# Two blocks moved into the paired stage, an early load, and two norms by halves in a two-layer sparse graph kernel

## The chip, the core and the metric

The kernel runs on one core of one Trainium2 chip. The metric is device time in microseconds for one execution. Five engines work side by side, each through its own queue in order: TensorE (PE in the profile), VectorE (DVE), ScalarE (ACT), GpSimd (POOL) and SyncE (SP). In this kernel SP issues the plain transfers, and POOL issues the indirect ones (gathers and scatters by row number). [...]

## What is computed

Two layers over 2708 nodes with 1024 features. Layer 0 is attention over each node's neighbours with a residual and a layer norm, layer 1 is a sum over neighbours, a projection, a residual and a layer norm.

```python
q = x @ W_q.T + b_q;  k = x @ W_k.T + b_k;  v = x @ W_v.T + b_v
z = (q @ k.T / sqrt(1024)) * adj
z = where(z == 0.0, -10000.0, z)
x = layernorm(x + relu(softmax(z) @ v))      # layer 0
x = layernorm(x + adj @ (x @ weight) + bias) # layer 1
```

The adjacency matrix is sparse and holds zeros and ones. A node without neighbours has the same value in every place of its row of z, so its attention is the plain mean over all nodes.

## The kernel before, in words

Everything is float32. The first stage lists each row's neighbours, sorts the rows by their number of neighbours, and folds the two weights of the scores into one matrix m, so that a score is the product of a row y = x m + constant with a row of x. Sorting makes 22 blocks of at most 128 rows, in two families (blocks 0 to 7 and 8 to 21). `SLOTS` (L32) gives for each sorted block how many neighbours its rows have at most: 15 in block 0, 11 in block 1, down to 0 in block 21, which is the list `last` (L98). Very connected rows are split into shares (the "hub").

**The y stage** (`y_block`, L288) goes over the rows in their natural order: 16 matmuls of 512 columns for a block of 128 rows, two additions on VectorE, a store to DRAM. Each block's part of xT comes by `load_x` (L272) into one of three buffers. Block 21 has only 20 rows. Its tile is cleared by GpSimd, then loaded (L278 to L280), and its products are laid out in four column groups (L305). ACT sums each block's columns (`column_sums`, L330) and from these sums comes the mean of x (L294).

**Attention jobs** (`attend`, `attend_one`, `attend_shares`) belong to sorted blocks. A job gathers the block's y rows (L343) and, slot by slot, neighbour rows of x (L349) into nine rotating tiles g, computes scores on VectorE (L792), a softmax, and the weighted sum of the same x rows in a tile r (L847, L849). A block that takes y rows from the second family needs the whole y stage to be over. The list `late_jobs` holds these.

**The projection of layer 0** turns r through PE (`flip`, L709, or `flip_shares`, L720, for block 0) and multiplies it with the 1024x1024 weight W_v. There are three ways. A single block ("v" step, `project`, L734) takes 16 matmuls of 512 columns. The mean (`project_mean`, L745) is one row for all rows of block 21. A pair of blocks ("p" step, `pair_products`, L990) takes seven products of half by half instead of eight, 28 matmuls in place of 32. For that it needs four combinations of the turned halves (`turn_pair`, L954, tile `s_all`) and the weight differences `wv_t`, four operations on VectorE (L1107 to L1110), the first of which changes a quarter of the weights in place. They lie in the buffers of m, so the y stage and the single projections of the original weights must come before them.

After the products, `finish0` (L879, single) or `finish_pair` (L1040) applies ReLU, adds the x row, and calls `norm` (L767): a mean from the accumulated sums, squares on ACT over the whole row (L775), Ln and Exp on ACT with four small VectorE operations for the inverse root, and the scaling of the row on ACT (L788). The row is scattered to the DRAM tensor x1 (L703). The tile t of a single block comes from the pool `wp` with two buffers; in a pair the first block's t comes from `wp`, the second's from a pool that opens when the y stage ends (`xb_pools[0]`), with two buffers too.

**The order** is written out by hand. `steps` (L1060) lists y blocks, single projections and pairs; the loop at L1090 walks through it, and a credit of estimated microseconds decides how many attention jobs are emitted before each step. A turn is emitted up to one step ahead of its projection (L1120). A scheduler then places instructions in the engines' queues by this order as their priority. `high_priority(URGENT)` marks the additions that free a PSUM bank. `follow` puts one instruction behind another, with a semaphore or, with `same=True`, only in the order of one engine's queue.

**Layer 1** starts when every row of x1 is scattered. `units` (L1192) lists one single block and ten pairs. `sum_rows` (L1197) gathers x1 rows (L349) and adds them up on VectorE (L1209, L1211), `turn1` turns them, `gather_x1` (L1214) fetches the residual row onto the bias, `work1` (L1235) multiplies and `finish1` (L1221) norms and scatters to the output. Before the loop, the sums of units 0, 1 and 2 are emitted, and in the loop those of unit i + 3.

```python
steps += [("v", b) for b in [1, 0] + last] + [("p", pair) for pair in pairs]
```

Of the kernel before, what the change touches and what calls it, by code (L numbers as in the profile page):

```python
# [20 lines left out]
P = 128  # L21
# [59 lines left out]
def sparse_part(ctx, tc, x, xT, adj, wqT, wkT, wvT, bq, bk, bv, w1, b1, out):  # L81
# [29 lines left out]
    with es:  # L111
# [158 lines left out]
        xts = []  # L270

        def load_x():  # L272
            b = len(xts)
            if b == NB:
                return
            r0, n = b * P, rows[b]
            xt = xa.tile([P, DC, P], F32, name="xt", bufs=3)
            if n < P:  # L278
                nc.gpsimd.memset(xt, 0.0)
            nc.sync.dma_start(out=xt[:, :, :n], in_=xT[:, r0:r0 + n].rearrange("(c p) n -> p c n", p=P))  # L280
            xts.append(xt)
# [48 lines left out]
        def column_sums(b, behind=None):  # L330
            for c in range(DC):
                put = nc.scalar.activation(junka, xts[b][:, c, :], AF.Copy, accum_out=xs[:, c, b:b + 1])  # L332
                if behind is not None and c % 2 == 0:
                    follow(put, behind[c // 2])
# [432 lines left out]
        def norm(t, sm, n, sm2=None):  # L767
# [21 lines left out]
            return end  # L789

        def score(yg, xg, s, n):
            nc.vector.scalar_tensor_tensor(junkv[:n], yg[:n, :D], scale, xg[:n], op0=ALU.mult, op1=ALU.mult,  # L792
                                           accum_out=s)
# [85 lines left out]
        def finish0(b, po, xr):  # L879
            n = rows[b]  # L880
            t = wp.tile([P, D], F32, name="t")
            for h in range(NH):
                hs = slice(h * HALF, (h + 1) * HALF)
                with tc.high_priority(URGENT):
                    nc.vector.tensor_add(t[:n, hs], po[h][:n], bias_bc[:n, hs])
            sm = stat.tile([P, 1], F32, name="sm")
            nc.vector.scalar_tensor_tensor(t[:n], t[:n], 0.0, xr[:n], op0=ALU.max, op1=ALU.add, accum_out=sm[:n])
            end = norm(t, sm, n)
            scatter(x1_d[:, :], b, n, t, "x1")
            return end  # L890
# [61 lines left out]


        def turn_pair(flips, pool):  # L954
# [12 lines left out]
            nc.vector.tensor_sub(S[2], a11, a21)  # L967
            nc.vector.tensor_sub(S[3], a12, S[1])
            return A, S
# [60 lines left out]
        def project_pair(pair, A, S):  # L1030
            ts = [(xb_pools[0] if k else wp).tile([P, D], F32, name="t", bufs=2) for k in range(2)]
            bias = halves_of(bias_bc)

            def whole(k, h, acc, what):
                add(halves_of(ts[k])[h], acc, what)

            pair_products(A, S, wv_q, wv_t, [bias, bias], [halves_of(t) for t in ts], whole, pair == pairs[-1])
            return ts

        def finish_pair(pair, ts):  # L1040
            for k, (b, t) in enumerate(zip(pair, ts)):
                xr, sums = pair_x[b], [stat.tile([P, 1], F32, name=f"sm{h}", bufs=6) for h in range(NH)]
                for h in (0, 1) if k == 0 else (1, 0):
                    th = halves_of(t)[h]
                    nc.vector.scalar_tensor_tensor(th, th, 0.0, halves_of(xr)[h], op0=ALU.max, op1=ALU.add, accum_out=sums[h])
                norm(t, sums[0], P, sums[1])
                scatter(x1_d[:, :], b, P, t, "x1")
# [7 lines left out]
        jobs = [6, 5, 4, 3, 2, 2, 1, 1, "hub", "hub", 0, 0, 0]  # L1055
        pairs = [(7, 20), (19, 18), (17, 8), (16, 11), (15, 10), (9, 14), (13, 12)]
        late_jobs = [7, 20, 8, 19, 18, 8, 17, 8, 16, 11, 15, 10, 20, 9, 14, 19, 13, 12, 18]
# [32 lines left out]
        for i, (kind, b) in enumerate(steps):  # L1090
# [105 lines left out]

        def sum_rows(b, k=0):  # L1197
            if b == "hub":
# [4 lines left out]
            for j in range(tab.shape[1] if b else J0):  # L1203
                if j == 0 and b not in [0, "hub"] + single + MIXED:
                    gather_slot(x1_d[:, :], tab[:n, 0:1], n, r)
                    continue
                xg = gather_slot(x1_d[:, :], tab[:n, j:j + 1], n, g_tile())
                if j == 0:
                    firsts.append(nc.vector.tensor_scalar(r[:n], xg[:n], ok[:n, 0:1], None, op0=ALU.mult))  # L1209
                else:  # L1210
                    nc.vector.scalar_tensor_tensor(r[:n], xg[:n], ok[:n, j:j + 1], r[:n], op0=ALU.mult, op1=ALU.add)  # L1211
            return r
# [8 lines left out]
        def finish1(b, t, sums):  # L1221

            n = rows[b]
            if sums is None:
                sums = [stat.tile([P, 1], F32, name=f"sm{h}", bufs=6) for h in range(NH)]
                for h in range(NH):
                    nc.scalar.activation(junks[:n, :HALF], halves_of(t)[h][:n], AF.Copy, accum_out=sums[h][:n])
            norm(t, sums[0], n, sums[1])
            scatter(out, b, n, t, "out")
# [5 lines left out]
        def work1(unit, A, S, xrs):  # L1235
# [4 lines left out]
            def whole(k, h, acc, what):  # L1240
                with tc.high_priority(URGENT):
                    nc.vector.scalar_tensor_tensor(halves_of(ts[k])[h], acc, 1.0, what, op0=ALU.mult, op1=ALU.add,
                                                   accum_out=sums[k][h])

            xs_ = [halves_of(xr) for xr in xrs]
# [357 lines left out]
```

## Time and profile before

| what | us |
|---|---|
| runs (three) | 1079.15, 1079.57, 1083.0 |
| median of the runs | 1079.57 |
| the profiled execution's own time | 1078.66 |
| its span in the profile | 1076.9 |

The profile's span runs from the first to the last recorded event; 1.8 us of the execution lie around it. The stages in the span, from the timeline of TensorE:

| stage | from | to | PE busy in it |
|---|---|---|---|
| lists, sorting, folding of the weights | 0 | 140 | |
| y stage with early attention | 140 | 522 | |
| singles 1 and 0, and the mean | 522 | 564 | |
| seven pairs of layer 0 | 564 | 758 | |
| from the last product of layer 0 to the first turn of layer 1 | 758 | 770 | 0.0 of 12 |
| layer 1's products | 770 | 1059 | |
| last norm, scatter, end | 1059 | 1077 | |

A row of a timeline gives the start and the length in us, the engine, the line of the code, the operation with output and inputs, and in brackets the idle time of the engine just before it with what ended it. A float32 matmul leaves two records on PE, so a count of records is twice the count of matmuls.

### The profile page before, as it was taken

How to read it: one execution, taken by the hardware profiler on the slowest of the kernel's cores; microseconds unless marked ns; L12 is line 12 of the kernel's file. 1: busy time of each engine (PE TensorE's matmuls, PEld its weight loads, DVE VectorE, ACT ScalarE, POOL GpSimd, SP SyncE). 2: the span in 40 equal slices, each digit the busy share in tenths (PEclk: the TensorE clock that was granted, in tenths of full speed). 3: DMA queues.
4: the chain of work that ended last, by engine and by line, in shares of the span. 5: the costliest groups of instructions: out<-in, count | busy, mean ns of one | idle time of the engine just before them, and what ended most of it. 6: DMA issues, size and time to landing. Idle time of an engine off the chain costs nothing.

```text
span 1076.9 us, 10217 instructions
## 1 busy us (share of the span) xinstructions
PE 1007.8 (94%) x2849; PEld 475.1 (44%) x2849; DVE 847.2 (79%) x1825; ACT 428.4 (40%) x898; POOL 490.7 (46%) x397
## 2 busy tenths in 40 slices
PE   7999999999998999999997999899489999999993
PEld 6444444444443444444543444444244444454441
DVE  8799999994388889998497999874578777887431
ACT  4688698422132332224433344332422363333322
POOL 1000140057564536435246566611477777887300
PEclk9999999999999999999998999999899999999997
DMA  9555457564886756796422677735589589969601
GB/s 355 199 206 203 173 196 273 170 244 125 300 279 225 240 191 189 229 334 198 149 92 86 205 255 268 235 118 193 167 284 256 199 269 324 293 204 329 179 39 42
DMA packets 90963, 229.20 MB, mean 213 GB/s; under 512 B 18410, under 2 KB 40394, under 8 KB 88188
## 3 DMA queue, kind: packets, MB, share of 16 engines
q0 software_dynamic: 48768, 148.05, 43.0%
q1 hardware_dynamic: 42128, 80.41, 21.7%
q8 instruction: 24, 0.39, 0.1%
q14 instruction: 43, 0.35, 0.1%
HBM read 219.61 MB, written 33.68 MB: 235 GB/s over the span
## 4 chain that ended last, share of the span: by engine, by line
PE 18%; issue 12%; DVE 11%; DMA 4%; POOL 3%; ACT 2%; POOLq 0%; DVEq 0%; ACTq 0%
PE po L976 16%; DVE junkv L792 2%; DVE r L849 2%; DMA g<-x_d,tabs 2%; DVE r L1211 1%; DMA yg<-y_d,tabs 1%; ACT junks L775 1%; DVE t L988 1%; POOL xr L343 1%; PE tr L716 1%; POOL g L349 1%; POOL x_d L703 1%; PE po L739 1%; PE tr L729 1%; POOL r L349 1%
## 5 line engine op out<-in xcount | busy, mean ns | idle before, releaser
L319 PE MATMUL po<-m_sb,xt 128*128 128x512 f32 x672 | 292.2, 594 | 3.3 <-DVE yo L323 3.3
L319 PEld LDWEIGHTS po<-m_sb,xt 128*128 128x128 f32 x672 | 126.4, 190 | 159.6 <-issue 150.8
L792 DVE SCALAR_TENSOR_TENSOR junkv<-yg,g 128x1024 uint8<-128x1024 f32 x109 | 133.1, 1221 | 36.3 <-DMA yg<-y_d,tabs 16.6
L349 POOL DMA_INDIRECT g<-in_x_dram,tabs x86 | 115.9, 1347 | 76.1 <-DVE r L849 19.4
L976 PE MATMUL po<-t,s_all 128*128 128x512 f32 x272 | 125.5, 604 | 10.9 <-DVE t L988 6.6
L1211 DVE SCALAR_TENSOR_TENSOR r<-g,valid,r 128x1024 f32<-128x1024 f32 x77 | 98.6, 1281 | 18.1 <-DMA g<-x_d,tabs 17.2
L609 PE MATMUL po<-wk_o,wq_o 128*128 128x512 f32 x256 | 110.5, 592 | 0.0
L775 ACT ACTIVATE junks<-t,lnm 128x1024 uint8<-128x1024 f32 (+1 forms) x43 | 49.3, 1146 | 135.2 <-DVE lnm L773 104.7
L739 PE MATMUL po<-wv,rT 128*128 128x512 f32 x224 | 97.7, 594 | 3.3 <-DVE pr L834 2.8
L976 PE MATMUL po<-w,rT 128*128 128x512 f32 x192 | 87.8, 607 | 0.0
L976 PEld LDWEIGHTS po<-t,s_all 128*128 128x128 f32 x272 | 52.0, 194 | 78.4 <-issue 60.7
L563 POOL DMA_INDIRECT tab_d<-rec,pos_i x22 | 27.1, 1230 | 129.9 <-DVE pos_i L552 123.5
L849 DVE SCALAR_TENSOR_TENSOR r<-g,pr,r 128x1024 f32<-128x1024 f32 x64 | 81.9, 1279 | 5.5 <-ACT r L861 4.6
L349 POOL DMA_INDIRECT g<-x_d,tabs x67 | 75.0, 1120 | 22.7 <-issue 15.5
L332 ACT ACTIVATE junka<-xt 128x128 f32<-128x128 f32 x176 | 53.8, 306 | 72.0 <-PE po L319 55.5
L788 ACT ACTIVATE t<-t,nmr,rstd 128x1024 f32<-128x1024 f32 (+1 forms) x43 | 52.6, 1238 | 73.8 <-DVE nmr L787 73.7
L224 DVE MAX8 few<-a 128x8 f32<-128x75 f32 (+3 forms) x132 | 79.2, 618 | 0.0
L609 PEld LDWEIGHTS po<-wk_o,wq_o 128*128 128x128 f32 x256 | 48.4, 190 | 59.3 <-issue 59.0
L976 PE MATMUL po<-w,s_all 128*128 128x512 f32 x160 | 72.1, 592 | 0.0
L221 DVE SCALAR_TENSOR_TENSOR a<-a,iota 128x2708 f32<-128x2708 f32 (+1 forms) x22 | 65.2, 2963 | 5.4 <-ACT junk L220 5.4
L739 PEld LDWEIGHTS po<-wv,rT 128*128 128x128 f32 x224 | 42.3, 190 | 56.3 <-issue 55.2
L219 ACT ACTIVATE junk<-a 128x2708 uint8<-128x2708 f32 (+1 forms) x22 | 54.1, 2459 | 24.7 <-DMA a<-in_adj_dram 20.1
(339 smaller groups left out, 1503.3 us busy)
## 6 DMA issues: line engine op xcount, KB each, us to landing
a<-in_adj_dram SPq DMA_DIRECT2D x21, 1354.0 KB, 5.9
xt<-in_xT_dram SPq DMA_DIRECT2D x21, 512.0 KB, 4.8
y_d<-yo SPq DMA_DIRECT2D x21, 512.0 KB, 5.7
g<-in_x_dram SPq DMA_DIRECT2D x21, 512.0 KB, 7.7
wq_i<-in_wqT_dram SPq DMA_DIRECT2D x8, 512.0 KB, 9.3
wk_i<-in_wkT_dram SPq DMA_DIRECT2D x8, 512.0 KB, 10.4
wv<-in_wvT_dram SPq DMA_DIRECT2D x16, 256.0 KB, 6.0
w<-in_w_dram SPq DMA_DIRECT2D x4, 1024.0 KB, 7.6
```

Source lines behind the costliest of these rows:

```text
L219: nc.scalar.activation(junk[:n], a[:n], AF.Sign, accum_out=cnt[:n, b:b + 1])
L221: nc.vector.scalar_tensor_tensor(a[:n], a[:n], 1.0, iota[:n], op0=ALU.is_equal, op1=ALU.mult)
L224: nc.vector.max(few[:n, i * 8:(i + 1) * 8], a[:n, cuts[i]:cuts[i + 1]])
L319: put = nc.tensor.matmul(po, xt[:, c, :], m_sb[c // 2][:, c % 2, k0:k1], start=(c == 0), stop=(c == DC - 1))
L349: nc.gpsimd.indirect_dma_start(out=dst[:n], out_offset=None, in_=src, in_offset=bass.IndirectOffsetOnAxis(ap=at, axis=0), bounds_check=N - ...
L609: nc.tensor.matmul(po, wq_o[i // 2][:, o, i % 2 * P:(i % 2 + 1) * P], wk_o[:, o, hs], start=(o == 0), stop=(o == DC - 1))
L739: put = nc.tensor.matmul(acc, rT[:, c, :], w[c // 4][h][:, c % 4, :], start=(c == 0), stop=(c == DC - 1))
L775: nc.scalar.activation(junks[:n], t[:n], AF.Square, bias=nm[:n], accum_out=vs[:n])
L792: nc.vector.scalar_tensor_tensor(junkv[:n], yg[:n, :D], scale, xg[:n], op0=ALU.mult, op1=ALU.mult, accum_out=s)
L849: nc.vector.scalar_tensor_tensor(r[:n], xg[j][:n], pr[:n, j:j + 1], r[:n], op0=ALU.mult, op1=ALU.add)
L976: put = nc.tensor.matmul(acc, a[:, k], w[:, k], start=start and k == 0, stop=stop and k == DC // 2 - 1, skip_group_check=True)
L1211: nc.vector.scalar_tensor_tensor(r[:n], xg[:n], ok[:n, j:j + 1], r[:n], op0=ALU.mult, op1=ALU.add)
```

## The change

It has these parts:

1. The last 20 rows of xT get a tile of their own, 32 columns wide, cleared by VectorE and loaded at the start of the stage that loads x. `load_x` returns that tile for the last block, and `column_sums` reads only its width.
2. Blocks 1 and 0 leave the single steps and become the first pair, (1, 0). The weight differences, emitted before the first pair, are therefore emitted before these two blocks. The turn of block 0 inside a pair joins its shares.
3. The tile t of the mean's block comes from the second pool, whose t gets three buffers.
4. The loop emits all of block 0's attention from step 13 on (before: step 15). The mean's turn is emitted only when the y stage is over.
5. The second block of layer 0's last pair (block 12) and the second block of layer 1's last unit (block 13) get a new norm, `norm_halves`: statistics of each half by `bn_stats`, joined by `bn_aggr`, and the scaling of one half on ACT and of the other on VectorE.
6. In layer 1 the sums of unit 2 are emitted in the loop, after the turn and the residual gathers of unit 1, and the first of them on VectorE stands behind the last combination of unit 1.

```diff
+        xt_last = xa.tile([P, DC, HUB], F32, name="xt_last", bufs=1)
+        nc.vector.memset(xt_last, 0.0)
+        nc.sync.dma_start(out=xt_last[:, :, :rows[-1]], in_=xT[:, (NB - 1) * P:].rearrange("(c p) n -> p c n", p=P))
...
+            if b == NB - 1:
+                xts.append(xt_last)
+                return
             xt = xa.tile([P, DC, P], F32, name="xt", bufs=3)
-            if n < P:
-                nc.gpsimd.memset(xt, 0.0)
...
+        def norm_halves(t, stats):
+            mv = stat.tile([P, 2], F32, name="mv")
+            nc.vector.bn_aggr(out=mv, in_=stats.rearrange("p h e -> p (h e)"))
+            lv = stat.tile([P, 1], F32, name="lv")
+            nc.scalar.activation(lv, mv[:, 1:2], AF.Ln, bias=eps)
+            near = stat.tile([P, 1], F32, name="near")
+            nc.scalar.activation(near, lv, AF.Exp, scale=-0.5)
...
+            nc.vector.scalar_tensor_tensor(nmr, mv[:, 0:1], -1.0, rstd, op0=ALU.mult, op1=ALU.mult)
+            applied.append(nc.scalar.activation(t[:, :HALF], t[:, :HALF], AF.Identity, bias=nmr, scale=rstd))
+            nc.vector.tensor_scalar(t[:, HALF:], t[:, HALF:], rstd, nmr, op0=ALU.mult, op1=ALU.add)
...
-            t = wp.tile([P, D], F32, name="t")
+            t = xb_pools[0].tile([P, D], F32, name="t", bufs=3) if b in [0] + last else wp.tile([P, D], F32, name="t")
...
-            ts = [(xb_pools[0] if k else wp).tile([P, D], F32, name="t", bufs=2) for k in range(2)]
+            ts = [(xb_pools[0] if k else wp).tile([P, D], F32, name="t", bufs=2 + k) for k in range(2)]
...
+                ends = half_stats() if k and pair == pairs[-1] else None
...
+                    if ends is not None:
+                        nc.vector.bn_stats(out=ends[:, h, :], in_=th)
-                norm(t, sums[0], P, sums[1])
+                if ends is None:
+                    norm(t, sums[0], P, sums[1])
+                else:
+                    norm_halves(t, ends)
...
-        pairs = [(7, 20), (19, 18), (17, 8), (16, 11), (15, 10), (9, 14), (13, 12)]
+        pairs = [(1, 0), (7, 20), (19, 18), (17, 8), (16, 11), (15, 10), (9, 14), (13, 12)]
...
-        steps += [("v", b) for b in [1, 0] + last] + [("p", pair) for pair in pairs]
+        steps += [("v", b) for b in last] + [("p", pair) for pair in pairs]
...
-            while 0 in jobs and i >= 15:
+            while 0 in jobs and i >= 13:
...
-                if k != "y" and c not in turned and not (left_y and k == "p"):
-                    turned[c] = turn0(c) if k == "v" else turn_pair([lambda rT, r=got[b_]: flip(r, rT) for b_ in c], xb_pools[0])
+                if k != "y" and c not in turned and not (left_y and (k == "p" or c in last)):
+                    turned[c] = turn0(c) if k == "v" else turn_pair([lambda rT, b_=b_, r=got[b_]: flip(r, rT) if b_ else flip_shares([got["hub"], r], rT) for b_ in c], xb_pools[0])
...
+                    if k and unit == units[-1]:
+                        if len(sums[k]) == NH:
+                            sums[k].append(half_stats())
+                        nc.vector.bn_stats(out=sums[k][-1][:, h, :], in_=halves_of(ts[k])[h])
...
-        got1[2] = [sum_rows(b, k) for k, b in enumerate(units[2])]
         for i, unit in enumerate(units):
...
+            if i == 0:
+                got1[2] = [sum_rows(b, k, halves_turned[-1]) for k, b in enumerate(units[2])]
```

`halves_turned` collects the last combination of every turned pair. `sum_rows` gets an argument `behind`, and puts its first VectorE operation behind it in VectorE's own order.

More of the change, by code (lines that the diff above doesn't have):

```diff
@@ L331, in column_sums @@
             for c in range(DC):
-                put = nc.scalar.activation(junka, xts[b][:, c, :], AF.Copy, accum_out=xs[:, c, b:b + 1])
+                put = nc.scalar.activation(junka[:, :xts[b].shape[2]], xts[b][:, c, :], AF.Copy, accum_out=xs[:, c, b:b + 1])
                 if behind is not None and c % 2 == 0:
@@ L789, in norm, with half_stats @@
             return end
+        def norm_halves(t, stats):
[5 more added lines that the diff above has]
+            nc.scalar.activation(near, lv, AF.Exp, scale=-0.5)
+            ve = stat.tile([P, 1], F32, name="ve")
+            nc.vector.scalar_tensor_tensor(ve, mv[:, 1:2], EPS, near, op0=ALU.add, op1=ALU.mult)
+            nc.vector.tensor_scalar(ve, ve, near, -0.5, op0=ALU.mult, op1=ALU.mult)
+            rstd = stat.tile([P, 1], F32, name="rstd")
+            nc.vector.scalar_tensor_tensor(rstd, ve, 1.5, near, op0=ALU.add, op1=ALU.mult)
+            nmr = stat.tile([P, 1], F32, name="nmr")
+            nc.vector.scalar_tensor_tensor(nmr, mv[:, 0:1], -1.0, rstd, op0=ALU.mult, op1=ALU.mult)
+            applied.append(nc.scalar.activation(t[:, :HALF], t[:, :HALF], AF.Identity, bias=nmr, scale=rstd))
+            nc.vector.tensor_scalar(t[:, HALF:], t[:, HALF:], rstd, nmr, op0=ALU.mult, op1=ALU.add)
+        def half_stats():
+            return stat.tile([P, NH, nc.vector.BN_STATS_DIM], F32, name="halves", bufs=2)
         def score(yg, xg, s, n):
@@ L951, in attend_shares @@
             yield
+        halves_turned = []
         def turn_pair(flips, pool):
@@ L967, in turn_pair @@
             nc.vector.tensor_sub(S[2], a11, a21)
-            nc.vector.tensor_sub(S[3], a12, S[1])
+            halves_turned.append(nc.vector.tensor_sub(S[3], a12, S[1]))
             return A, S
@@ L1195, in sparse_part, with sum_rows @@
         firsts = []
-        def sum_rows(b, k=0):
+        def sum_rows(b, k=0, behind=None):
             if b == "hub":
@@ L1208, in sum_rows @@
                 if j == 0:
-                    firsts.append(nc.vector.tensor_scalar(r[:n], xg[:n], ok[:n, 0:1], None, op0=ALU.mult))
-                else:
-                    nc.vector.scalar_tensor_tensor(r[:n], xg[:n], ok[:n, j:j + 1], r[:n], op0=ALU.mult, op1=ALU.add)
+                    put = nc.vector.tensor_scalar(r[:n], xg[:n], ok[:n, 0:1], None, op0=ALU.mult)
+                    firsts.append(put)
+                else:
+                    put = nc.vector.scalar_tensor_tensor(r[:n], xg[:n], ok[:n, j:j + 1], r[:n], op0=ALU.mult, op1=ALU.add)
+                if behind is not None:
+                    follow(put, behind, same=True)
+                    behind = None
             return r
@@ L1227, in finish1 @@
                     nc.scalar.activation(junks[:n, :HALF], halves_of(t)[h][:n], AF.Copy, accum_out=sums[h][:n])
-            norm(t, sums[0], n, sums[1])
+            if len(sums) == NH:
+                norm(t, sums[0], n, sums[1])
+            else:
+                norm_halves(t, sums[-1])
             scatter(out, b, n, t, "out")
```

## The prediction

> **What bounds the kernel now.** I read the page's busy times first, then TensorE's own timeline for its waits, then the timelines of the engines that those waits name.
>
> ```profile
> PE 1007.8 (94%) x2849; PEld 475.1 (44%) x2849; DVE 847.2 (79%) x1825; ACT 428.4 (40%) x898; POOL 490.7 (46%) x397
> ```
>
> PE is busy 1007.8 of 1076.9 us, so time comes from its 69 us of gaps or from fewer matmuls. One float32 matmul of 512 columns leaves two records; eight records take 3.43 us from start to start. A block alone is 32 records (13.7 us), a pair 56 (24.0 us). The gaps that the change touches, in PE's timeline (start, us, engine, line; in brackets the idle time and its releaser):
>
> ```profile
> 512.42 3.67 PE L305 MATMUL po<-m_sb,xt 128*32 128x257 f32 x64 [1.29 <-DMA xt<-in_xT_dram]
> ...
> 584.12 6.08 PE L976 MATMUL po<-t,s_all 128*128 128x512 f32 x8 [6.60 <-DVE t L988]
> ```
> ```profile
> 801.66 3.70 PE L976 MATMUL po<-t,s_all 128*128 128x512 f32 x8 [2.99 <-DVE xr L988]
> ```
>
> The middle one is the largest. VectorE and GpSimd before it:
>
> ```profile
> 583.37 1.29 DVE L988 TENSOR_TENSOR t<-po,bias_bc 128x512 f32<-128x512 f32 x2 [6.90 <-DMA x_d<-t,tabs]
> ```
> ```profile
> 569.87 7.48 POOL L349 DMA_INDIRECT g<-in_x_dram,tabs  x1 [0.30 <-DVE rstd L785]
> 577.65 0.94 POOL L343 DMA_INDIRECT xr<-in_x_dram,tabs  x1 [0.30 <-issue]
> 578.89 1.00 POOL L703 DMA_INDIRECT x_d<-t,tabs  x1 [0.30 <-issue]
> ```
>
> The first pair's tile t needs the buffer of block 0's t. That is free once its scatter has landed (583.3), and the scatter (578.89) stood on POOL's queue behind a gather of 7.48 us. Then the clock (columns of a stretch: PE, PEld, DVE, ACT and POOL busy, PEclk, DMA share, GB/s):
>
> ```profile
> 582.00:584.00 2.00, 0.00 (x0) 0.00 (x0) 0.63 (x2) 0.00 (x0) 0.00 (x0) 0.53 0.31 109
> 584.00:586.00 2.00, 1.89 (x3) 0.85 (x4) 2.00 (x5) 0.00 (x0) 0.00 (x0) 0.50 0.00 0
> ```
>
> **The change, part by part** (negative is a gain)
>
> *Last rows in a tile of their own.* The x transfer is issued at 506.17 behind POOL's memset (505.17) and a buffer; PE waits 1.29 us for it. Issued hundreds of microseconds earlier, it is there. The new memset is 256 elements a partition on VectorE, and the sums of these rows shrink from 128 to 32 columns on ACT, neither on the path. **-1.29.** Next behind it is y's own matmul stream, which has no gap.
>
> *Blocks 1 and 0 as a pair.* 64 records become 56: **-3.43** of PE. VectorE pays: four more combinations (0.60 apart), three more additions from PSUM (7 instead of 4, 0.60), halved ReLU passes (+0.3): 4.5 us.
>
> *The stall at 584.* The mean's t goes to the other pool with a third buffer, and the pair (1, 0) takes one from each. So pair (7, 20) waits for block 2's t, scattered long before. The gap (6.60) goes. What it did to the clock goes too: the eight records from 584.12 took 6.08 us, the same group at 592.61 took 3.60, so 2.48. The Trainium skill (TensorE: Matmul & The Clock Gate, What's actually happening) says that an idle window of some 3.4 us halves the clock and some 3.4 us of work restore it, a loss of 1.7 (my estimate from the page): by it the stall is worth 8.3, by the row 9.08. The row decides; it also shows 2.99 us at 798.7 without such a loss (3.70 for eight records). **-9.08.** Late next is the t of the pair before last, as in all later pairs, which show no such wait.
>
> *The weight differences move ahead of pair (1, 0).* Four operations of 2.27 to 2.29 us (9.1). Before, blocks 1 and 0 covered them. Now PE has from y's end: flip of block 1 1.04, flip of shares 3.55, x-mean broadcast 0.90, mean's products 3.66, and the pair's first 16 records, which need no difference, 6.9: 16 us. VectorE's chain is the mean's end (9.2 at the latest, since q12 is changed in place), then 2.29 + 2.28 = 13.8. The combinations fit before, in the idle time that ends at 530.18 (4.61 before that row). Cover 2 us: nothing lost if the differences go first, 1.8 lost if the three row sums of blocks 7, 20 and 19 (1.28 each) do. Between 0 and +4 I take **+1**.
>
> Here a rule speaks against the change. The Trainium skill (SBUF — State Buffer, SBUF: two separate sides) says that a VectorE instruction with two SBUF inputs and a GpSimd instruction that reads SBUF exclude each other. By it POOL issues nothing during differences and combinations, 11.5 us, just when it should fetch y rows and x rows for the late blocks. The gather of 7.48 us above lay beside two differences (570.67 to 575.2). But beside layer 1's differences (775.8 to 782.6) gathers came through, one for each:
>
> ```profile
> 777.04 1.89 POOL L349 DMA_INDIRECT r<-x_d,tabs  x1 [0.30 <-issue]
> 779.24 2.02 POOL L349 DMA_INDIRECT g<-x_d,tabs  x1 [0.30 <-issue]
> 781.57 2.48 POOL L343 DMA_INDIRECT xr<-x_d,tabs  x1 [0.30 <-issue]
> ```
>
> By the rule the late blocks begin 11.5 us later, by these rows about 4 (four gathers at 2.1 plus 0.3 instead of 1.0 plus 0.3). The rows are nearer: same operation and size, a queue full of gathers. In the sum the rule gives the last rival's 1081.4, the rows the forecast.
>
> *VectorE's lead.* Late scores and sums lose 9.1 (differences first) and 4.5 (pairing), and win the idle time around the stall. They show in PE as flips that wait for row sums: now 2.43, 0.43, 0.82 and 0.17 at 682.7, 687.6, 707.3 and 713.7, and 0.39 for an addition. But the flips of pair (9, 14) run at 682 and 687 and its combinations at 707: 20 us of slack. Between 0 and +7 I take **+1.5**.
>
> *Block 0's attention two steps earlier.* Its gathers pass the row constants on the SP queue and the g tiles. Three waits of VectorE (5.67, 1.22, 4.38 in 508 to 522) take the displaced work: 0; without them a row load late for y, +1.3 at most, as the last rows' now.
>
> *Norms by halves.* At the end now:
>
> ```profile
> 1058.84 0.69 DVE L1242 SCALAR_TENSOR_TENSOR t<-po,xr 128x512 f32<-128x512 f32 x1 [2.02 <-PE po L976]
> ```
> ```profile
> 1059.82 1.15 ACT L775 ACTIVATE junks<-t,lnm 128x1024 uint8<-128x1024 f32 x1 [2.95 <-DVE lnm L773]
> ...
> 1062.49 1.24 ACT L788 ACTIVATE t<-t,nmr,rstd 128x1024 f32<-128x1024 f32 x1 [0.87 <-DVE nmr L787]
> ```
>
> From 1059.46 to Ln's start (1061.09) are 1.63 us: small operation, squares, read-out. Instead: statistics of one half, no row; nearest is another pass over 128x512, 0.69; aggregation like a small operation, 0.21; hand-over 0.1: 1.0. It saves 0.6. The last pass over 1024 (1.24) becomes two of 512 side by side, ACT about 0.7: saves 0.55. **-1.15** at the end, and as much (**-1.2**) after block 12, whose scatter (763.64) gates layer 1's gathers (767.21). Were the statistics twice as long, 0.5 each; a gain above 1.5 is excluded, since Ln, Exp and four small operations stay.
>
> *Third sums later.* Layer 1's POOL then fetches x1 rows of blocks 19 and 18 (now 781.57 and 784.35) ahead of four gathers, and VectorE makes unit 1's combinations (787.53) before the sums of 17 and 16. It should shorten the wait of 2.99: the addition at 800.91 stood behind sums that waited for transfers. But the four gathers come later by two transfers, about 3 us, while the DMA share is 1.0. Between -3.5 and +2 I take **-1.5**.
>
> Sum: -1.29 -3.43 -9.08 +1 +1.5 -1.2 -1.5 -1.15 = -15.15. From the profiled execution's 1078.66 (span 1076.9 and 1.8 around it) this gives **1063.5 us**; the runs' median, 1079.57, is 0.9 higher, which the range takes in.
>
> **Rivals**
>
> *VectorE becomes the bound of late layer 0.* For: it is busy 24.71 and 24.89 of 25 us in 600 to 650. Against: it is busy only 21.68 of 44 us in 714 to 758. Then layer 0 wins only what VectorE wins: 1.3 earlier y, 7.6 idle in 577 to 600, 2 of the idle time before 530, less 4.5: 6.4. With -3.85 behind it: 1068.4.
>
> *The wait moves to the front.* Row sums and late scores go ahead of the differences, and PE waits at the pair's third product 6 us, 2.5 for the clock: 1 becomes 8.5, 1071.
>
> *Slower: POOL starves.* If the rule of the shared port holds fully at y's end, POOL issues nothing for 11.5 us. VectorE then idles some 8 us after the three sums, the late blocks stay that late, and two waits of PE pass the length that halves the clock (2.5 each): 13 against the first rival's gain of 10.25: 1081.4. It decides from 10.3 us of such losses on. For it speaks the row of 7.48; against it the rows of 1.89 to 2.48, and gathers for 7, 20 and 19 issued before y's end (500 to 508).
>
> **How the numbers follow.** Forecast 0.58, VectorE bound 0.22, wait in front 0.12, POOL starved 0.08. The forecast's own ends are 1059 (no new stall, third sums -3.5) and 1068. The range reaches down to 1057 for a stall at 876 (1.92 us behind ACT) that a shifted order may remove, and up to 1072 for the first two rivals. About 0.5% of this kernel, 5.4 us, can be told from no change. Faster 0.87, same 0.06, slower 0.07.
>
> **What would show it.** No idle before L305. No gap above 3 us and PEclk 1.0 between y's end and pair (7, 20)'s end. No L739 records for blocks 1 and 0: 160 in place of 224, and 56 more of L976. Differences before late scores, with POOL's gathers beside them near 2 us: were they above 4, the third rival is at work. Waits of PE's flips for row sums above 10 us in all before the last pair: VectorE bound. Scatter to out 4.0 us after the last L1242 starts, 5.2 now.

## The result and the profile after

The changed kernel takes 1069.86 us (median of 1068.75, 1068.89, 1070.82 and 1071.41), the kernel before 1079.86 beside it. The ratio is 0.9903, with a 95% interval from 0.9878 to 0.9928: faster by 10.0 us (7.8 to 13.2), where 15.15 were predicted. The profiled execution took 1068.75, its span is 1067.0 (before 1076.9). In set 1 of the experiments below every kernel took longer, the one before too (1093.87 us; 1079.82 and 1079.31 in sets 2 and 3), some 10 us of it before the first single projection, so of that set only ratios and stage lengths are read.

I cut both spans at the same marks: the start of the first single projection (L739 before, L744 after), the end of the last rows' products (L305, L310), the end of layer 0's last product, layer 1's first turn and last product.

| stretch | before | after | difference | predicted |
|---|---|---|---|---|
| start to first single projection | 334.5 | 333.7 | -0.8 | 0 |
| to the end of the last rows' products | 181.6 | 188.0 | **+6.4** | -1.3 |
| to the end of layer 0's last product | 241.7 | 227.1 | **-14.6** | -10.0 |
| TensorE's gap between the layers | 12.5 | 11.7 | -0.8 | -1.2 |
| layer 1's first turn to last product | 288.5 | 289.2 | +0.7 | -1.5 |
| last addition to the issue of its scatter | 5.16 | 4.41 | -0.75 | -1.15 |

The rest of the span is the same within 0.1. So the ten microseconds are mainly a gain of 14.6 that I had put too low, less a loss of 6.4 that I had not seen; the small rows bring 1.7 together. The page of the changed kernel, engines' busy time:

```profile
PE 1006.7 (94%) x2841; PEld 473.5 (44%) x2841; DVE 854.1 (80%) x1843; ACT 425.1 (40%) x894; POOL 488.6 (46%) x396
```

PE lost only 1.1 us of work although 3.4 went with eight records, in part because some of the same matmuls ran longer at a lower clock. TensorE's timeline of the changed kernel at the end of y (start, length, engine, line, operation; in brackets the idle time and its releaser):

```profile
477.88 0.29 PE L960 MATMUL tr<-ident,nm 128*128 128x128 f32 x1 [1.29 <-DVE nm L939]
...
510.76 0.38 PE L970 MATMUL mm<-den,tops 128*128 128x1 f32 x2 [2.32 <-DVE den L966]
511.01 7.09 PE L324 MATMUL po<-m_sb,xt 128*128 128x512 f32 x12
518.03 3.67 PE L310 MATMUL po<-m_sb,xt_last 128*32 128x257 f32 x64
521.63 6.28 PE L324 MATMUL po<-m_sb,xt 128*128 128x512 f32 x14
529.82 0.62 PE L190 MATMUL tr<-ident,xbT 128*128 128x128 f32 x4 [1.91 <-DVE xbT L300]
```

Read it from below. L310 has no bracket: the wait of 1.29 us for the last rows is gone. But two waits stand ahead of it, at L960 and L970. They are a transpose and a matmul of the join of block 0's shares (`attend_shares`); a transpose leaves one record, a product two. Before the change the matmul stood behind y's last product and waited for nothing:

```profile
523.00 0.28 PE L944 MATMUL mm<-den,tops 128*128 128x1 f32 x2
```

TensorE's matmuls run in the order of its queue here: while L970 waits for `den`, the y products behind it, which need nothing of it, wait too. The twelve records behind it took 7.09 instead of 5.15 (3.43 for eight), and the clock row shows why (columns: PE, PEld, DVE, ACT, POOL busy, PEclk, DMA share, GB/s):

```profile
510.00:515.00 5.00, 4.24 (x8) 1.92 (x9) 0.98 (x8) 1.32 (x7) 0.00 (x0) 0.73 0.67 270
```

Not all of the 6.4 is the join's. The stage's first projection, too, ran at a lower clock than before (0.68 granted in 333 to 338; before, 1.00 in 334 to 339) and took 1.70 us longer (before, then changed):

```profile
334.47 13.97 PE L739 MATMUL po<-wv,rT 128*128 128x512 f32 x32 [2.79 <-DVE pr L834]
```
```profile
333.71 15.67 PE L744 MATMUL po<-wv,rT 128*128 128x512 f32 x32 [2.08 <-DVE pr L860]
```

The runs below show both lengths with the join early and with it late, so this part comes by chance. The stage adds up to -1.29 for the last rows, +3.61 for the two waits, +1.94 for the clock behind L970 and +1.70 here: 5.96 of the 6.4.

Why `den` was late, from the timelines of ScalarE and VectorE in the changed kernel:

```profile
506.18 0.29 ACT L854 ACTIVATE pr<-scores,nms 128x2 f32<-128x2 f32 x1 [8.45 <-DVE nms L845]
...
506.48 0.29 ACT L337 ACTIVATE junka<-xt 128x128 f32<-128x128 f32 x1
...
510.15 0.19 ACT L337 ACTIVATION_READ_ACCUMULATOR junka<-xt 128x1 f32 x1
510.24 0.28 ACT L965 ACTIVATE turn<-nm,top 128x1 f32<-128x1 f32 x1
```
```profile
508.20 0.28 DVE L963 TENSOR_REDUCE top<-tops 128x1 f32<-128x128 f32 x1
...
510.55 0.16 DVE L966 TENSOR_TENSOR den<-den,turn 128x1 f32<-128x1 f32 x1 [1.65 <-ACT turn L965]
```

`top` is ready at 508.5, but ScalarE, which had stood 8.45 us behind another block's scores, first takes the column sums that had piled up (506.48 to 510.24) before it comes to the join's activation.

Behind y the change does what it should. Pair (7, 20) starts at 568.53 with no bracket, and no wait of the pairs before the last is above 1.2 us (before, the longest for a row sum was 2.43; its row is the last one here):

```profile
568.53 4.03 PE L1004 MATMUL po<-wv,rT 128*128 128x512 f32 x9
...
623.39 1.06 PE L721 MATMUL tr<-ident,r 128*128 128x128 f32 x8 [0.48 <-DVE r L875]
678.43 1.06 PE L721 MATMUL tr<-ident,r 128*128 128x128 f32 x8 [0.47 <-DVE r L875]
702.11 1.07 PE L721 MATMUL tr<-ident,r 128*128 128x128 f32 x8 [1.14 <-DVE rden L859]
```
```profile
682.70 1.06 PE L716 MATMUL tr<-ident,r 128*128 128x128 f32 x8 [2.43 <-DVE pr L834]
```

The differences, in VectorE's timeline, and GpSimd's gathers beside them:

```profile
532.37 2.29 DVE L1141 TENSOR_TENSOR wv<-wv,wv 128x2048 f32<-128x2048 f32 x1 [2.70 <-PE po L757]
534.70 2.29 DVE L1142 TENSOR_TENSOR t<-wv,wv 128x2048 f32<-128x2048 f32 x1
...
548.51 2.27 DVE L1143 TENSOR_TENSOR t<-t,wv 128x2048 f32<-128x2048 f32 x1
```
```profile
533.45 2.04 POOL L348 DMA_INDIRECT yg<-y_d,tabs  x1 [0.30 <-issue]
...
548.18 3.43 POOL L348 DMA_INDIRECT xr<-in_x_dram,tabs  x1 [1.94 <-DVE t L913]
```

The first two, the ones that the pair's third product needs, come first; three row sums stand between them and the others, and TensorE waits for none of the four.

### The profile page after: what moved, and what is told of

Read it like the earlier page. It is cut to its first block, busy times and chain, and to the rows that moved or that the text cites. A ratio compares the mean times of both kernels' runs of the same rounds, so it can differ in the third digit from the quotient of the medians.

```text
span 1067.0 us, 10202 instructions
## 1 busy us (share of the span) xinstructions
PE 1006.7 (94%) x2841; PEld 473.5 (44%) x2841; DVE 854.1 (80%) x1843; ACT 425.1 (40%) x894; POOL 488.6 (46%) x396
## 4 chain that ended last, share of the span: by engine, by line
DVE 33%; PE 29%; issue 15%; DMA 11%; POOL 8%; ACT 3%; POOLq 0%; DVEq 0%; ACTq 0%
PE po L1004 21%; DVE junkv L818 5%; DVE few L224 5%; DVE a L221 5%; DMA g<-x_d,tabs 4%; DVE r L875 4%; POOL g L354 3%; DMA g<-in_x_dram,tabs 3%; PE po L614 2%; PE po L324 2%; DVE t L1016 2%; POOL tab_d L568 1%; PE tr L721 1%; DMA yg<-y_d,tabs 1%; DMA g<-in_x_dram,tab 1%
## 5 line engine op out<-in xcount | busy, mean ns | idle before, releaser
L354 POOL DMA_INDIRECT g<-in_x_dram,tabs x86 | 105.9, 1231 | 77.8 <-DVE r L875 22.0
L1004 PE MATMUL po<-t,s_all 128*128 128x512 f32 x288 | 131.8, 599 | 3.6 <-DVE xr L1016 3.6
L354 POOL DMA_INDIRECT g<-x_d,tabs x67 | 83.7, 1249 | 22.7 <-issue 14.0
L780 ACT ACTIVATE junks<-t,lnm 128x1024 uint8<-128x1024 f32 (+1 forms) x41 | 47.0, 1145 | 109.0 <-DVE lnm L778 94.3
L1004 PEld LDWEIGHTS po<-t,s_all 128*128 128x128 f32 x288 | 54.7, 192 | 72.6 <-issue 62.5
L793 ACT ACTIVATE t<-t,nmr,rstd 128x1024 f32<-128x1024 f32 (+1 forms) x41 | 50.2, 1238 | 87.6 <-DVE nmr L792 87.4
L337 ACT ACTIVATE junka<-xt 128x128 f32<-128x128 f32 x168 | 51.4, 306 | 73.6 <-PE po L324 57.7
L744 PE MATMUL po<-wv,rT 128*128 128x512 f32 x160 | 71.3, 604 | 2.1 <-DVE pr L860 2.1
L1004 PE MATMUL po<-t,rT 128*128 128x512 f32 x144 | 64.8, 593 | 1.4 <-DVE t L1283 1.4
```

What stands on the lines that cost most here:

```text
L337: put = nc.scalar.activation(junka[:, :xts[b].shape[2]], xts[b][:, c, :], AF.Copy, accum_out=xs[:, c, b:b + 1])
L354: nc.gpsimd.indirect_dma_start(out=dst[:n], out_offset=None, in_=src, in_offset=bass.IndirectOffsetOnAxis(ap=at, axis=0), bounds_check=N - ...
L744: put = nc.tensor.matmul(acc, rT[:, c, :], w[c // 4][h][:, c % 4, :], start=(c == 0), stop=(c == DC - 1))
L1004: put = nc.tensor.matmul(acc, a[:, k], w[:, k], start=start and k == 0, stop=stop and k == DC // 2 - 1, skip_group_check=True)
```

## The experiments

Stage lengths of all runs, from one profile each, in us; the ratio to the kernel before of the same set, with its interval:

| run | y (to the last rows' products) | late layer 0 | layer 1 | ratio |
|---|---|---|---|---|
| before | 181.6 | 241.7 | 288.5 | 1 |
| changed | 188.0 | 227.1 | 289.2 | 0.9903 (0.9878 to 0.9928) |
| c_after (set 2) | 188.7 | 226.9 | 290.0 | 0.9896 (0.9881 to 0.9910) |
| e1_join15 (set 1) | 182.0 | 228.7 | 292.9 | 0.9853 (0.9820 to 0.9886) |
| c_join15 (set 3) | 182.0 | 228.7 | 290.8 | 0.9851 (0.9833 to 0.9868) |
| e5_join13_alone (set 1) | 189.5 | 241.0 | 296.2 | 1.0031 (1.0012 to 1.0051) |
| e2_mean_t (set 1) | 181.7 | 231.6 | 291.4 | 0.9927 (0.9899 to 0.9955) |
| e4_sums_early (set 1) | 187.5 | 228.5 | 294.5 | 0.9922 (0.9893 to 0.9950) |
| e3_whole_norms (set 2) | 186.7 | 228.5 | 290.5 | 0.9901 (0.9887 to 0.9915) |
| e6_xt_alone (set 2) | 182.1 | 236.9 | 290.4 | 0.9956 (0.9941 to 0.9970) |
| e8_late_unit3 (set 2) | 180.3 | 226.9 | 286.3 | 0.9842 (0.9829 to 0.9854) |
| c_late_unit3 (set 3) | 182.0 | 228.1 | 290.5 | 0.9839 (0.9824 to 0.9855) |
| e9_mean_early (set 3) | 180.3 | 225.3 | 290.8 | 0.9824 (0.9798 to 0.9850) |

Two losses of clock, 1.7 us each, explain most of the scatter in the first two columns. The first projection takes 15.67 in place of 13.97 in the changed kernel, c_after, e1_join15, c_join15, e6_xt_alone and c_late_unit3. The mean's products take 5.35 in place of 3.66 in e1_join15, c_join15, e3_whole_norms, e4_sums_early and c_late_unit3. And one profile need not be typical: that of e5_join13_alone took 1105.01 us against a median of 1097.51, that of e8_late_unit3 1058.58 against 1062.14.

**The join, put back.**

```diff
-            while 0 in jobs and i >= 13:
+            while 0 in jobs and i >= 15:
```

> The changed kernel with one number put back: block 0's attention is emitted from step 15 on, as before, and no longer from step 13. My theory: the join of its shares, which has matmuls and turns of its own on TensorE, moved with it into the y stage and made y end at 527.9 in place of 522.3. With step 15 y's last product starts about 507 to 509 without the two waits in front of it (1.29 and 2.32 us) and with eight-record groups at full clock; y ends 3.5 to 5.6 earlier, and the run takes 1064 to 1066.5. Rival (the y stage is longer for the other edits, such as the early load on the SP queue or the sums of the last rows on ScalarE): y still ends at 527 to 528 and the time stays within 1 us of 1069.9. Second rival (the join has to be paid at one place or the other): y ends at 522, but the turn of block 0 for the pair (1, 0) then waits for the shares by as much, and the time stays at 1069 to 1070.

The y stage is 182.0 long in place of 188.0, and the ratio falls from 0.990 to 0.9853, which of 1079.86 would be 1064.0. Run again beside others in a later set:

> The changed kernel with block 0's attention emitted from step 15 on, run again beside the next two. With y's end some 6 us earlier than in the changed kernel and nothing given back in late layer 0: 0.984 to 0.986 of the time before, against 0.990 for the changed kernel. If the join's cost only moved, 0.989 to 0.991.

1063.9 us, ratio 0.9851. In TensorE's timeline of this run the join's matmuls have no bracket:

```profile
504.84 0.28 PE L970 MATMUL mm<-den,tops 128*128 128x1 f32 x2
504.98 0.30 PE L960 MATMUL tr<-ident,nm 128*128 128x128 f32 x1
505.12 7.89 PE L324 MATMUL po<-m_sb,xt 128*128 128x512 f32 x18
...
522.65 0.28 PE L970 MATMUL mm<-den,tops 128*128 128x1 f32 x2
524.73 0.62 PE L190 MATMUL tr<-ident,xbT 128*128 128x128 f32 x4 [1.79 <-DVE xbT L300]
525.28 5.35 PE L757 MATMUL po<-wv,mean 128*32 128x256 f32 x64
```

The second L970 is back behind y's last product, and no longer waits. The first rival falls: y is 6.0 us shorter with this one line put back and every other edit kept. Of the second rival a part came: late layer 0 is 1.6 to 1.8 longer, because the mean's products took 5.35 us (3.66 in the changed kernel), but most of the join's cost is gone. Against the changed kernel run once more,

> The changed kernel once more, unchanged, as the measure for the other runs of this set: 0.990 of the time before, as in the first comparison (0.9878 to 0.9928). If the first runs hold, y's last product ends 6 us later after the first single projection than in the kernel before, and from y's end to the end of layer 0 it takes some 14.6 us less.

which took 1068.62 (ratio 0.9896), step 15 is worth 4.7 us in medians (1063.9 against 1068.62), 4.2 with each set's own kernel before set against it, 4.9 by the ratios. The traces agree: 6.0 to 6.7 less in y, 1.6 to 1.8 more behind it.

**The join moved, alone, in the kernel before.** The same line, 15 to 13, nothing else.

> The kernel before, with block 0's attention emitted from step 13 on and nothing else changed. My theory: its join's matmuls stand in TensorE's queue inside the y stage and wait for VectorE and ScalarE there; y ends 4 to 6 us later than 522.3. Whether the end of the kernel follows is open, because the gap at 584 hangs on GpSimd's queue and on block 0's norm: 1083 to 1085 if the gap stays 6.6, about 1079 if block 0's scatter comes earlier and the gap shrinks by what y lost. Rival (the y stage was longer for another edit): y ends within 1 us of 522.3 and the time within 1 us of 1079.6.

y grows to 189.5, late layer 0 stays at 241.0, and the kernel is 3.4 us slower (0.0031 of 1093.87; interval 1.3 to 5.6), as expected for a gap that stays, though y's growth of 7.9 is more than the 4 to 6 expected. TensorE's timeline of this run:

```profile
489.95 0.29 PE L934 MATMUL tr<-ident,nm 128*128 128x128 f32 x1 [2.91 <-DVE nm L913]
...
522.83 0.59 PE L944 MATMUL mm<-den,tops 128*128 128x1 f32 x2 [2.32 <-DVE den L940]
523.28 8.46 PE L319 MATMUL po<-m_sb,xt 128*128 128x512 f32 x12
...
603.73 5.79 PE L976 MATMUL po<-t,s_all 128*128 128x512 f32 x8 [6.57 <-DVE t L988]
```

The same two waits come without any other edit, the first longer (2.91 in place of 1.29), and with them a larger loss of clock (8.46 for twelve records, 7.09 in the changed kernel). The large gap later is as long as before (6.57). So the loss belongs to the step that moved the join. For its size this profile, 7.5 us above the median of its kernel, is no measure.

**The mean's tile, alone, in the kernel before.**

```diff
-            t = wp.tile([P, D], F32, name="t")
+            t = xb_pools[0].tile([P, D], F32, name="t", bufs=3) if b in last else wp.tile([P, D], F32, name="t")
...
-            ts = [(xb_pools[0] if k else wp).tile([P, D], F32, name="t", bufs=2) for k in range(2)]
+            ts = [(xb_pools[0] if k else wp).tile([P, D], F32, name="t", bufs=2 + k) for k in range(2)]
```

> The kernel before, with the mean's t alone taken from the second pool, with three buffers there. Nothing else is changed: blocks 1 and 0 stay single, the differences stay where they were. My theory: the gap of 6.60 us at 584 and the 2.48 us that the clock loses after it are both due to this one buffer; both go and nothing takes their place, 1070 to 1072 (9.1 less than before). Rival (VectorE is what late layer 0 hangs on, so a gap closed early opens again as later waits for row sums): the gap goes, but the waits of TensorE's flips for row sums from 620 to 715 grow from 4.2 to 8 us or more, and the time is 1074 to 1077.

The ratio, 0.9927, is 8.0 us (4.9 to 11.0) of 1093.87. Late layer 0 is 9.4 us shorter than in e5_join13_alone of the same set, which has that stage as before. The first pair runs through, at full clock:

```profile
577.86 4.46 PE L976 MATMUL po<-wv,rT 128*128 128x512 f32 x10
582.15 3.60 PE L976 MATMUL po<-t,s_all 128*128 128x512 f32 x8
```

The later waits for row sums are 1.27, 0.21, 0.30 and 1.27, less than the 4.2 of before, so VectorE doesn't take the gap back and the rival is out. My price for the stall, 9.08, lies in the interval.

**The last rows' tile, alone, in the kernel before.** The first hunk of the change, with `load_x` and the width of the column sums.

> The kernel before, with nothing but the last rows' own tile, loaded early. As predicted: the wait of 1.29 us ahead of these products is gone and y ends 1.3 earlier, time 1.3 less if the end follows. Rival (the gap at 584 hangs on GpSimd's queue, not on y's end, and takes the 1.3 back): y ends 1.3 earlier, the gap grows from 6.6 to 7.9, and the time is the same as before within 0.5 us.

1075.85 us, ratio 0.9956, so 4.8 us less (3.2 to 6.4): more than either expected. The wait ahead of these products is gone; the gap is 6.79 in place of 6.60. TensorE's first single projection lost 1.7 us of clock here (15.67 for 32 records in place of 13.97), so y is not shorter in this profile. What else is missing is in late layer 0: waits of 0.74 and 0.18 for row sums where before had 4.2 in all, and 5.16 us instead of 6.08 for the eight records after the gap. Why the row sums came earlier I can't say from one profile; e2's waits, 3.05 in all, show that this sum moves from kernel to kernel without a cause that I named.

**Whole norms again, in the changed kernel.** `ends = None` in `finish_pair`, and the four lines of `bn_stats` in `whole` of layer 1 left out.

> The changed kernel with the norms of the two last blocks taken whole again, as before. As predicted, halves gain 1.2 at the boundary of the layers and 1.15 at the end, so this run would be 2.35 us slower than the changed kernel. By the reading of its trace they gain 0.78 and 0.75: TensorE's gap between the layers is 12.4 to 12.5 in place of 11.7, and from the last product's addition to the issue of the last scatter it takes 5.2 in place of 4.4; the run is 1.5 slower. Rival (the clock of layer 1's first products, or transfers, swallow what the boundary gains): 0.75 slower.

In the traces the theory holds within 0.01. The gap between the layers is 12.45 (c_after 11.68), and from the last addition to the scatter's issue it takes 5.16 (1053.50 to 1058.66) against 4.41. The times, 1069.43 against 1068.62, are 0.8 apart, which is less than their intervals: what the two norms bring is read from the traces, 0.77 and 0.75, and that the time follows in full is not shown. The end of the changed kernel (VectorE, ScalarE, GpSimd):

```profile
1049.74 0.69 DVE L1283 SCALAR_TENSOR_TENSOR t<-po,xr 128x512 f32<-128x512 f32 x1 [1.43 <-PE po L1004]
...
1050.47 0.69 DVE L1288 BATCH_NORM_STATS2 halves<-t 128x6 f32<-128x512 f32 x1
1051.20 0.21 DVE L799 BATCH_NORM_AGGREGATE mv<-halves 128x2 f32<-128x12 f32 x1
...
1052.84 0.81 ACT L811 ACTIVATE t<-t,nmr,rstd 128x512 f32<-128x512 f32 x1 [0.86 <-DVE nmr L810]
1052.84 0.55 DVE L812 TENSOR_SCALAR t<-t,rstd,nmr 128x512 f32<-128x512 f32 x1
...
1054.15 0.95 POOL L708 DMA_INDIRECT out_dram<-t,tabs  x1 [5.16 <-ACT t L811]
```

**The third sums early again, in the changed kernel.** The line of `got1[2]` goes back ahead of the loop, without `behind`.

> The changed kernel with the sums of layer 1's third unit (blocks 19 and 18, by name the unit after the first pair) emitted ahead of the loop again, as before. As predicted, the later emission gains 1.5 us, so this run would be 1.5 slower than the changed kernel, 1071.4. By the reading of the two traces it gains nothing: from layer 1's first turn to its last product 289.2 us against 288.5 before, so this run would be within 0.8 us of 1069.9, or up to 0.7 faster. Which wait is there is also told apart: if the wait of 3.16 us at 792.7 comes from the order of these sums, it changes by more than 1 us; if it comes from gathers that are late at this point in either order, it stays near 3.

(The third unit is blocks 17 and 16; the expectation names the wrong pair.) The ratio, 0.9922, can't be told from the changed kernel's 0.9903 and 0.9896. The wait at the first pair's third product is there in this order too:

```profile
805.18 2.08 PE L1004 MATMUL po<-t,s_all 128*128 128x512 f32 x2 [4.68 <-DVE xr L1016]
```

With these sums later it is 3.16 in the changed kernel, 2.29, 3.03 and 2.91 in c_after, e3_whole_norms and c_join15, 4.20 in e1_join15. But there a second wait stands just ahead of it, at the turn of blocks 17 and 16, for the sums that now come late (c_after):

```profile
784.25 1.06 PE L721 MATMUL tr<-ident,r 128*128 128x128 f32 x8 [1.85 <-DVE r L1246]
```

It is 1.45 to 1.85 in c_after, e1, e3 and c_join15 and 0.17 in the changed kernel; with early sums no trace has it (before, e2, e4, e6). So the later order moves part of the wait to the turn. Layer 1 takes 288.5 and 290.4 with early sums (before, e6) and 289.2 to 290.8 with later ones (changed, c_after, e3, c_join15), outside set 1. No gain shows. By the ratios e4 is 2.0 to 2.8 us slower, but their intervals allow some 4 us either way, so the predicted 1.5 is neither shown nor excluded.

**Layer 1's later sums behind the addition that TensorE waits for**, with step 15:

```diff
-            if i + 3 < len(units):
+            if i > 1 and i + 3 < len(units):
                 got1[i + 3] = [sum_rows(b, k) for k, b in enumerate(units[i + 3])]
...
+            at_add = len(adds)
             pending = list(zip(unit, *work1(unit, *turned1.pop(i), xrs.pop(i))))
+            if i == 1:
+                got1[3], got1[4] = [[sum_rows(b, k, adds[at_add]) for k, b in enumerate(units[u])] for u in (3, 4)]
```

Here `adds` collects the additions of `add`.

> The changed kernel with block 0's attention emitted from step 15 on, and in layer 1 the sums of the units after the third put behind, on VectorE, the addition that TensorE waits for at the first pair's third product. Join part: 6 us less before y's end. Layer 1 part, theory: the wait there (3.16 in the changed kernel, 4.20 with step 15 alone) comes from the order of VectorE's queue, where this addition stands behind sums that wait for gathers; it falls under 1 us, the clock stays full after it, and layer 1 takes 3 to 5 less: in all 0.981 to 0.984 of the time before. Rival (layer 1's front is bound by its transfers): the wait moves to the turn of the fourth unit or to later row sums, and the run stays at 0.985 to 0.986, as with step 15 alone.

1062.14, ratio 0.9842. The third product no longer waits, and layer 1's 286.3 looked like the theory. But this profile is of an execution 3.6 us below the median, and in it, too, TensorE waits two products further on:

```profile
792.33 3.70 PE L1004 MATMUL po<-t,s_all 128*128 128x512 f32 x8 [1.74 <-DVE xr L1016]
```

Beside step 15 alone, in set 3, the time does not look like the theory:

> Step 15 and layer 1's later sums behind the first pair's addition, run again beside the run with step 15 alone. Theory (order of VectorE's queue makes the wait): 2 to 4 us less than step 15 alone, and layer 1's first turn to last product 286 to 287 in place of 289 to 291. Rival (transfers bound layer 1's front, the first run was a good one): within 1 us of step 15 alone.

1063.19 against 1063.9, layer 1 290.5 against 290.8. TensorE and VectorE of this run:

```profile
785.90 3.60 PE L1004 MATMUL po<-t,s_all 128*128 128x512 f32 x8
789.34 3.60 PE L1004 MATMUL po<-w,s_all 128*128 128x512 f32 x8
796.50 3.78 PE L1004 MATMUL po<-t,s_all 128*128 128x512 f32 x4 [3.56 <-DVE xr L1016]
```
```profile
787.43 1.28 DVE L1246 SCALAR_TENSOR_TENSOR r<-g,valid,r 128x1024 f32<-128x1024 f32 x1 [4.00 <-DMA g<-x_d,tabs]
789.97 1.28 DVE L1246 SCALAR_TENSOR_TENSOR r<-g,valid,r 128x1024 f32<-128x1024 f32 x1 [1.26 <-DMA g<-x_d,tabs]
```

The wait is there again, two products further, at the next addition behind the same sums, which wait for gathers while the DMA share is 1.0 (785 to 795). It is longer than in e8_late_unit3 (3.56 for 1.74), and the eight records behind it took 6.34 us (3.70 there), which is nearly all that layer 1 differs by between the two profiles. The rival holds as far as these two runs go: the wait changes its place, and no gain in time shows.

**The mean's column sums early**, on top of that: the last rows' eight sums are taken in y block 18 (`NB - 4`), not behind the last products.

```diff
+            if b == NB - 4:
+                xts_last_sums()
             if b == NB - 1:
-                column_sums(b)
...
+        def xts_last_sums():
+            for c in range(DC):
+                nc.scalar.activation(junka[:, :HUB], xt_last[:, c, :], AF.Copy, accum_out=xs[:, c, NB - 1:NB])
```

> As the run before it, and the column sums of the last rows, which have had their own tile since the start, are taken on ScalarE four y blocks earlier instead of behind the last one. Since the mean is now the first thing after y, TensorE waits 1.8 us for it at y's end. Theory: eight sums of 0.35 us go from ScalarE's path there, the wait falls below 0.2, and the run is 1.6 us faster than the one before it. Rival (the weight differences, which cannot start before the mean's products are done, or late layer 0's row sums set the pace): the wait goes and comes back at the pair's third product or at later turns, gain under 0.5.

1060.54, ratio 0.9824, the fastest of all: 2.7 us less than the run before it in medians and 1.6, the theory's figure, by the ratios; the intervals overlap, so the gain is not certain. Late layer 0 is 225.3 in place of 228.1 and 226.9. TensorE's timeline at y's end, without a bracket:

```profile
518.78 1.45 PE L324 MATMUL po<-m_sb,xt 128*128 128x512 f32 x3
520.17 3.66 PE L760 MATMUL po<-wv,mean 128*32 128x256 f32 x64
```

## Why the prediction was right, and where it was not

The time lies in the range (1057 to 1072), but 6.4 above the forecast, and the sum reached it mainly through two errors of opposite sign. By its own steps:

- **Last rows in a tile of their own, -1.29.** The wait is gone. e6_xt_alone gained more (4.8), partly by waits elsewhere that I can't assign.
- **Pairing, -3.43, and VectorE's lead, +1.5.** The matmuls went as counted. The waits for row sums and additions before the last pair fell from 4.2 to 2.1 instead of growing by 1.5. The 20 us of slack that I had seen at 682 to 707 fit this; I then charged for it all the same. These 3.6 us are the larger part of what late layer 0 won beyond the forecast (14.6 for 10.0); why the sums came earlier is not shown.
- **The stall, -9.08.** Right. e2_mean_t alone brings 8.0 in time (interval 4.9 to 11.0) and 9.4 in its stage.
- **Differences ahead of the pair, +1.** No product waits for them. What I had not seen is the mean's broadcast, now first behind y: it waits 1.91 us for column sums (L190 at 529.82), which block 1's flip and first products covered before. So +1 was charged for the wrong reason, and 1.91 came.
- **Block 0's attention two steps earlier, 0. This is the step that failed.** I followed its gathers and VectorE's work, and not its join, which has two transposes and two small matmuls on TensorE's in-order queue. They cost 1.29 + 2.32 of waiting and 1.94 of clock, 5.55 in the trace, and 4.2 to 4.9 in the time by c_after and c_join15. The other 1.70 that y lost is the first projection's clock. With this step undone and all others kept, the kernel takes 1063.9, and the forecast was 1063.5. That the two meet so closely is luck: the row sums came out 3.6 better than charged, and the third sums, the norms and the mean's wait together some 3.2 worse.
- **Norms by halves, -1.2 and -1.15.** Right in kind, measured 0.77 and 0.75. From the last addition's end to Ln it takes 1.01 us (1050.43 to 1051.44), as estimated. Mis-sized was the end: the pass over a half takes 0.81 on ScalarE, not 0.7, and from its end to the scatter's issue it takes 0.50 (1053.65 to 1054.15) where the whole pass had 0.27 (1063.73 to 1064.00).
- **Third sums later, -1.5.** No gain is shown. Part of the wait that it should shorten went to the turn of the same sums, and the additions that wait stand behind sums that wait for gathers (c_late_unit3).

The rivals: VectorE is busy 24.71 of 25 us in 545 to 570 of the changed kernel, yet TensorE waits for it 2.1 us in all, so it isn't the bound. No wait moved to the pair's third product; from y's end to the end of pair (7, 20) the longest wait is the mean's 1.91, and the clock is 1.00 (528 to 593). GpSimd was not starved: gathers of 2.04 and 3.43 beside the differences.

## What to carry to other kernels

When a piece of work is emitted earlier, list its instructions on every engine, and look first for the small ones on the engine that sets the end: a transpose and a matmul of 0.3 us each held up a queue of ready ones for 3.6 us. Where an engine waits for gathers that come late, reordering what stands behind them may only move the wait, as it did in layer 1 here. A total that comes out near the forecast can hide two errors; dividing both traces at the same marks shows them.

## What was not expected of the hardware

A short wait of TensorE sometimes costs a second time. The same kernel ran as e8_late_unit3 and as c_late_unit3, with nearly the same waits (1.96 and 2.44 ahead of the first projection, 1.79 and 1.79 at y's end). TensorE's timelines of the first and of the second:

```profile
334.31 13.97 PE L744 MATMUL po<-wv,rT 128*128 128x512 f32 x32 [1.96 <-DVE pr L860]
...
523.24 3.66 PE L757 MATMUL po<-wv,mean 128*32 128x256 f32 x64
```
```profile
334.18 15.67 PE L744 MATMUL po<-wv,rT 128*128 128x512 f32 x32 [2.44 <-DVE pr L860]
...
524.81 5.35 PE L757 MATMUL po<-wv,mean 128*32 128x256 f32 x64
```

In the second the first projection and the mean's products each took 1.7 us longer, and the clock granted in 525 to 530 of its trace was 0.66. The Trainium skill (TensorE: Matmul & The Clock Gate, What's actually happening) ties the low clock to an idle window of some 3.4 us; here a loss followed a wait of 1.79 in one run and none a wait of 2.79 in another (the kernel before at 334.47, 13.97 for 32 records), and 2.44 here and 2.45 in e2_mean_t (13.97) went both ways. So the length of the wait does not decide it; what does, no run shows. A wait of about 2 us at these places costs 2 or 3.7, and two profiles of one kernel may differ by some 1.7 us for each such place. That is one more reason to remove short waits, and to compare medians.
